# Keeping the adapted feed-forward weights in DRAM for their second use, and splitting the last expert block around the attention before it

## The chip, the core and the metric

The kernel runs on one core of a Trainium2 chip. The metric is the device time of one execution in microseconds, as the median of several runs. All arithmetic is fp32.

## The reference

The kernel computes two layers of a transformer on `x` of 2 x 512 tokens with 512 channels. Each step adds a block of the normalised input to `x`:

```python
x = x + latent_attention_small(layernorm(x))
x = x + ffn_lora(layernorm(x))      # first pass
x = x + gqa(layernorm(x))
x = x + ffn_lora(layernorm(x))      # second pass, the same weights
x = x + mla(layernorm(x))
x = x + ffn_moe(layernorm(x))       # first pass
x = x + mha(layernorm(x))
x = x + ffn_moe(layernorm(x))       # second pass, the same weights
```

Two of the blocks matter here. The feed-forward block with adapters is

```python
y = x @ weight.T + bias
lo = (x @ A[adapter].T) @ B[adapter].T      # rank 16; the adapter depends on the batch alone
out = y + where(use_lora, lo, 0)
```

As the adapter depends on the batch alone, the kernel adds the product of the two adapter matrices to the weight, once for each of the two batches, and multiplies by that sum. The expert block is

```python
logits = x @ W_router.T                      # 8 experts
probs = softmax(logits); top 2, scaled to sum 1 -> combine (tokens x 8)
h  = einsum('nd,erd->ner', x, A)             # 8 experts x rank 16 = 128 columns
hw = h * combine[:, :, None]
out = x @ W_base.T + b_base + 2 * einsum('ner,eor->no', hw, B)
```

## The kernel before

**Tiling.** `x` stays in SBUF as eight tiles of 128 tokens, `x0` to `x7`; tiles 0 to 3 are batch 0 and 4 to 7 batch 1 (`NT` is 4, `NTILES` 8, `KC` 4 chunks of 128 channels). `layernorm(t)` takes statistics on DVE, an inverse root on POOL (L210, tile `rstd`), the scaled rows `xn` on DVE (L182, two buffers), four transposes on TensorE (L195) and a copy by ACT (L200) into `xT[batch]`. With a `bias` it also issues an addition of the bias to `x[t]` on POOL (L215), after `xn`. Most matrix products go through `chain` (L162), a run of matmuls that accumulate in one PSUM bank. The sums are added to `x` on DVE (L218).

**Banks.** PSUM has eight banks by four names: three `sc`, two `pj`, two `tp` and one `av`. `proj()` takes the `pj` banks in turn, `tr()` the `tp` banks, `sc()` the `sc` banks; `turn()` goes round all of them. A bank can be taken again when the last reader of its tile is done.

**Weights.** Tags of the pool `w` are rings: `w8` has five buffers of 1 MB, `w3` six of up to 384 KB, `bias` one. Loads go through SyncE's queue (SP) in the order of the program; a load waits until the buffer that it is to fill is free, and those behind it wait too.

**The adapted block.** `AdaptedBlock` (L736 on) loads the weight, both adapter matrices and the bias; `adapt(m)` makes one quarter of the adapted weight for both batches: two matmuls of 48 rows by 512 columns (L761) and two additions on DVE (L765). `product(b, t)` is the chain of four matmuls of one token tile. In the first pass the four calls of `adapt` stand in the list `ending` at the end of `attn_latent_small`, between the last steps of that attention; that attention's TensorE order is written by hand. The second pass, `ffn_lora`, makes a second `AdaptedBlock` and adapts again.

**The expert block.** `ffn_moe` is called twice, with loads of its own each time. `front(t)` is a chain of four matmuls of 136 columns into a `pj` bank (128 columns of `h` and the 8 logits) followed by the router's chain: 16 small operations on DVE, from `nmax` (L1360) to `hw` (L1378), with an exponential on ACT (L1362) after the first. The last of them, `hw`, reads the bank. `back(t)` transposes `hw` (L1389), copies it with ACT (L1391), and runs a chain of five 512-column matmuls into an `sc` bank. The loop does `front(t)`, a piece of other work, `layernorm` and `back(t - 1)`. The second call writes the output rows.

**The last attention.** `attn_mha` goes over the two batches: `prepare(b)` projects q and k (`rotated`, four chains each into `pj` banks, followed by ACT L1534, a shuffle and a multiplication on DVE L1536 and L1537, two operations on POOL L1538 and L1539, and scattering DMAs) and the values (four chains into `sc` banks); `core(b)` does scores, softmax, the weighted sum and the output product. `core` stands in a branch on a register. In `prepare(1)` the order of the instructions on each engine is the scheduler's; in `core` TensorE's is written by hand. After `prepare(1)` tiles 0 to 3, which are final by then, are normalised for the second expert block.

Of the kernel before, what the change touches and what calls it, by code (L numbers as in the profile page):

```python
# [31 lines left out]
F32 = mybir.dt.float32  # L32
# [5 lines left out]
B, S, D = 2, 512, 512  # L38
P = 128
NT = S // P  # L40
KC = D // P
# [4 lines left out]
class Block:  # L46


    def __init__(self, ctx, tc, x, out):
        nc = self.nc = tc.nc  # L50
        self.tc = tc
        self.out = out
        pool = lambda name, bufs, **kw: ctx.enter_context(tc.tile_pool(name=name, bufs=bufs, **kw))
        self.const = pool("const", 1)
        self.w = pool("w", 2)
        self.work = pool("work", 2)
        self.small = pool("small", 6)
        self.psum = pool("psum", 2, space=bass.MemoryType.PSUM)
        self.turns = 0
        self.held = None  # L60
        self.coef = None

        self.x = [
            self.const.tile([P, D], F32, tag=f"x{t}", name=f"x{t}") for t in range(NTILES)
        ]
        self.source = x
        self.load_x(0)


        self.room = self.const.tile([P, 4 * KC * S], F32, tag="room", name="room")  # L70
# [313 lines left out]
def attn_latent_small(k, a):  # L384
# [7 lines left out]
    nc, tc = k.nc, k.tc  # L392
    with ExitStack() as ctx:
        lp = ctx.enter_context(tc.tile_pool(name="a", bufs=2))
# [260 lines left out]
        blocks = []  # L655
        last = len(quartets) - 1
        adapt = [lambda m=m: blocks[0].adapt(m) for m in range(KC)]
        feed = [lambda t=t: blocks[0].product(0, t) for t in range(NT)]

        tokens = [lambda t=t: k.layernorm(t, k.turn, back=True) for t in range(NT)]  # L660
# [77 lines left out]
class AdaptedBlock:  # L738
# [5 lines left out]
    def __init__(self, k, a):  # L744
        self.k = k
        self.w = k.load(a["f0_w"], [P, KC, D], "w8", 5)

        self.la = k.load(a["f0_a"], [P, D], "w3", 6)
        self.lb = k.load(a["f0_b"], [P, D], "w3", 6)
        self.bias = k.load_row(a["f0_bias"], D, "bias")  # L750
        k.nc.vector.tensor_scalar(self.la, self.la, k.coef, None, ALU.mult)
        self.adapted = [
            k.w.tile([P, KC, D], F32, tag="w8", name="adapted", bufs=5) for b in range(B)
        ]

    def adapt(self, m):
        k, nc = self.k, self.k.nc
# [13 lines left out]
        k.add_to_x(b * NT + t, ps)  # L771


def ffn_lora(k, a):


    block = AdaptedBlock(k, a)
    for m in range(KC):
        block.adapt(m)
    for t in range(NT):  # L780
        k.add_bias(t, block.bias)
    for b in range(B):
        for t in range(NT):
            block.product(b, t)
            if b == 0:
                k.layernorm(NT + t, k.turn, bias=block.bias)
            else:
                k.layernorm(t, k.turn, back=True)
# [533 lines left out]
        k.release()  # L1322


def ffn_moe(k, a, last=False, beside=lambda t: None):

    nc, tc = k.nc, k.tc
    E, R = 8, 16  # L1330
    with ExitStack() as ctx:
        lp = ctx.enter_context(tc.tile_pool(name="f1", bufs=3))
        w = k.load(a["f1_w"], [P, KC, D], "w8", 5)
        war = k.load(a["f1_ar"], [P, KC, E * R + E], "w3", 6)
        wb = k.load(a["f1_b"], [P, D], "w3", 6)
        bias = k.load_row(a["f1_bias"], D, "bias")
        order = k.load_row(a["c_order"], E, "c_order")

        for t in range(NT):
            k.add_bias(t, bias)  # L1340

        def best(p, name):

            top = k.sm(1, name)
            nc.vector.tensor_reduce(top, p, AX.X, ALU.max)
            cand = lp.tile([P, E], F32, tag="cand", name="cand")
            nc.vector.scalar_tensor_tensor(cand, p, top, order, ALU.is_equal, ALU.mult)
            first = k.sm(1, "first")
            nc.vector.tensor_reduce(first, cand, AX.X, ALU.max)
            hot = lp.tile([P, E], F32, tag="hot" + name, name="hot" + name)  # L1350
            nc.vector.tensor_scalar(hot, cand, first, None, ALU.is_equal)
            return top, hot

        def front(t):
            b, cols = t // NT, bass.ts(t % NT, P)
            ps = k.proj()
            k.chain(ps[:, : E * R + E], [(k.xT[b][:, c, cols], war[:, c]) for c in range(KC)])
            logits = ps[:, E * R : E * R + E]
            nmax = k.sm(1, "nmax")
            nc.vector.tensor_reduce(nmax, logits, AX.X, ALU.max, negate=True)  # L1360
            p = lp.tile([P, E], F32, tag="p", name="p")
            nc.scalar.activation(p, logits, AF.Exp, bias=nmax, scale=1.0)  # L1362
            p1, hot1 = best(p, "p1")
            rest = lp.tile([P, E], F32, tag="rest", name="rest")
            nc.vector.scalar_tensor_tensor(rest, hot1, -2.0, p, ALU.mult, ALU.add)
            p2, hot2 = best(rest, "p2")
            both = k.sm(1, "both")
            nc.vector.tensor_tensor(both, p1, p2, ALU.add)
            inv = k.sm(1, "inv")
            nc.vector.reciprocal(inv, both)  # L1370
            c1 = lp.tile([P, E], F32, tag="c1", name="c1")
            nc.vector.tensor_scalar(c1, hot1, p1, None, ALU.mult)
            c2 = lp.tile([P, E], F32, tag="c2", name="c2")
            nc.vector.scalar_tensor_tensor(c2, hot2, p2, c1, ALU.mult, ALU.add)
            comb = lp.tile([P, E], F32, tag="comb", name="comb")
            nc.vector.tensor_scalar(comb, c2, inv, 2.0, ALU.mult, ALU.mult)
            hw = lp.tile([P, E, R], F32, tag="hw", name="hw")
            nc.vector.tensor_tensor(  # L1378
                hw,
                ps[:, : E * R].rearrange("p (e r) -> p e r", e=E),  # L1380
                comb.unsqueeze(2).broadcast_to([P, E, R]),
                ALU.mult,
            )
            return hw

        def back(t, hw):
            b, cols = t // NT, bass.ts(t % NT, P)
            tp = k.tr()
            nc.tensor.transpose(tp[:, :P], hw.rearrange("p e r -> p (e r)"), k.ident)  # L1389
# [8 lines left out]
        rows = {}  # L1398
        for t in range(NTILES + 1):
            if t < NTILES:  # L1400
                rows[t] = front(t)
                beside(t)
            if t < NT:
                k.layernorm(NT + t, bias=bias)
            if t > 0:
                back(t - 1, rows.pop(t - 1))
            if t > NT and not last:
                k.layernorm(t - 1 - NT)


class CausalBound:
# [79 lines left out]
        pool.memset(self.nm[i // 4][:, i % 4], 0.0)  # L1491


def attn_mha(k, a, exact, rooms):

# [8 lines left out]
    with ExitStack() as ctx:  # L1504
# [43 lines left out]
        def prepare(b):  # L1548
            rotated(b, wq, bq, q, (nc.sync, nc.sync))
            if b == 0:  # L1550
                for t in range(NT, NTILES):
                    k.layernorm(t, bias=bo)
            last = rotated(b, wk, bk, kk, (nc.sync, nc.scalar))

            with tc.issue_after(last):
                values(b)
# [135 lines left out]

        for b in range(B):
            prepare(b)
            if b:

                for t in range(NT):
                    k.layernorm(t)
            with tc.If(exact != 0) as branch:
                core(b, True)  # L1700
            with branch.Else():
                core(b, False)
# [3 lines left out]
def kernel(ctx: ExitStack, tc: tile.TileContext, a: dict, out: bass.AP):  # L1706
# [2 lines left out]
    block = attn_latent_small(k, a)  # L1709
    bound = CausalBound(k, a)  # L1710
    attn_gqa(k, a, bound, block)
    ffn_lora(k, a)
    attn_mla(k, a)
    with k.tc.tile_pool(name="heads", bufs=1) as pool:
        rooms = HeadRooms(k, a, pool)
        ffn_moe(k, a, beside=rooms.fill)
        attn_mha(k, a, bound.register(), rooms)
    ffn_moe(k, a, last=True)

# [154 lines left out]
```

## Time and profile before

| what | us |
|---|---|
| median of 3 runs | 2096.95 |
| lowest and highest | 2095.71, 2101.05 |
| the profiled execution, its own time | 2095.05 |
| the profiled execution, span from first to last instruction | 2093.0 |

The mean granted clock of TensorE in that execution is 0.992 of full speed. In the profile PE is TensorE's matmuls, PEld its weight loads, DVE the vector engine, ACT the scalar engine, POOL GpSimd and SP the queue of SyncE. A timeline row gives the start, the duration, the engine, the line of the kernel, the operation, output and inputs by the program's names, the shapes and the number of merged records; in brackets stands how long the engine was idle before and what released it. An fp32 matmul leaves two records, so a chain of four is shown as x8. A row of waits gives the engine and line that waited, what it waited for, the total in us, how often, and the longest.

### The profile page before, as it was taken

To read this page: it belongs to the slowest core of one execution; us is meant where nothing else is said; L and a number is where in the kernel's file an instruction comes from. 1 tells how busy PE (TensorE), PEld (TensorE's weight loads), DVE (VectorE), ACT (ScalarE), POOL (GpSimd) and SP (SyncE) were. 2 spreads that over 40 slices of the span, in tenths; PEclk is the share of its full clock that TensorE was granted. 3 is DMA by queue.
4 is the path that set the end of the run, shared out by engine and by line. 5 is a ranking of instruction groups with operands and counts; after the bars stand their busy time and mean duration, and the time that the engine had idled before them with its cause. 6 is when DMAs were issued, how large, how long until landed. Compare 5 with 4: busy or idle time off the path is not lost. (4 is left out here: it accounts for less than half of the span.)

```text
span 2093.0 us, 40127 instructions
## 1 busy us (share of the span) xinstructions
PE 2028.5 (97%) x15560; PEld 1152.4 (55%) x15560; DVE 1354.0 (65%) x3575; ACT 741.2 (35%) x2072; POOL 969.1 (46%) x1239
## 2 busy tenths in 40 slices
PE   9999999999999999999999989999999989999998
PEld 5544435666666566666665534545454444554654
DVE  6788756656665466566765556666666784846845
ACT  1665632222232222222232145444544311541631
POOL 1101026675656467666653256555555545215220
PEclk9999999999999999999999999999999999999999
DMA  3001022222222222222220321010101003002001
GB/s 110 6 21 41 1 71 71 76 72 71 91 73 77 84 71 76 77 93 77 74 75 20 117 62 55 21 54 22 51 22 52 2 6 71 2 2 41 2 2 41
DMA packets 70220, 107.43 MB, mean 51 GB/s; under 512 B 13698, under 2 KB 50690, under 8 KB 63236
## 3 DMA queue, kind: packets, MB, share of 16 engines
q1 hardware_dynamic: 69380, 103.71, 15.8%
q8 instruction: 126, 2.06, 0.4%
q10 hardware_dynamic: 640, 1.05, 0.3%
q14 instruction: 74, 0.61, 0.1%
HBM read 80.61 MB, written 2.10 MB: 40 GB/s over the span
## 5 line engine op out<-in xcount | busy, mean ns | idle before, releaser
L263 ACT ACTIVATE room<-room,nmax 128x128 f32<-128x128 f32 (+3 forms) x384 | 212.1, 554 | 483.5 <-DVE nmax L253 482.1
L274 POOL TENSOR_SCALAR room<-room,invs 128x128 f32<-128x128 f32 (+3 forms) x384 | 197.4, 533 | 142.2 <-DVE invs L271 142.2
L314 PE MATMUL sc<-turned,vals 32*128 32x128 f32 (+7 forms) x1034 | 187.9, 415 | 1.3 <-DVE turned L287 1.3
L314 PE MATMUL pj<-turned,vals 32*128 32x384 f32 (+7 forms) x708 | 186.6, 425 | 0.0
L210 POOL TENSOR_TENSOR rstd<-ve,mhalf 128x1 f32<-128x1 f32 x80 | 45.6, 574 | 249.6 <-DVE ve L208 230.8
L314 PE MATMUL tp<-turned,vals 32*128 32x256 f32 (+7 forms) x770 | 149.0, 423 | 3.0 <-DMA vals<-v 2.1
L242 PE MATMUL sc<-kT,q 128*32 128x256 f32 (+4 forms) x1528 | 134.0, 384 | 6.8 <-DVE invs L271 4.1
L287 DVE STREAM_TRANSPOSE turned<-room 128x1152 f32<-128x1152 f32 x80 | 109.1, 1363 | 42.1 <-POOL room L274 39.8
L314 PEld LDWEIGHTS sc<-turned,vals 32*128 32x128 f32 (+1 forms) x1034 | 120.3, 168 | 14.4 <-issue 4.4
L958 POOL TENSOR_TENSOR q<-q,cosq 128x512 f32<-128x512 f32 x60 | 89.4, 1489 | 60.2 <-DVE t L955 60.2
L162 PE MATMUL sc<-w,room 128*128 128x512 f32 (+1 forms) x256 | 112.3, 583 | 0.0
L314 PEld LDWEIGHTS pj<-turned,vals 32*128 32x128 f32 (+1 forms) x708 | 104.7, 170 | 4.1 <-issue 1.6
L314 PEld LDWEIGHTS tp<-turned,vals 32*128 32x128 f32 (+1 forms) x770 | 98.2, 170 | 11.5 <-issue 5.7
L218 DVE TENSOR_TENSOR x<-sc,x 128x512 f32<-128x512 f32 x79 | 54.2, 686 | 74.5 <-PE sc L162 69.6
L162 PE MATMUL sc<-w,ctxT 128*128 128x512 f32 x224 | 101.5, 596 | 0.0
L568 PE MATMUL sc<-qm,keys 32*128 32x512 f32 x206 | 96.8, 628 | 0.0
L274 POOL TENSOR_SCALAR probs<-probs,invs 128x128 f32<-128x128 f32 (+3 forms) x128 | 65.7, 532 | 64.7 <-DVE invs L271 60.8
L242 PE MATMUL tp<-kT,q 128*32 128x512 f32 (+4 forms) x984 | 91.7, 407 | 3.8 <-DVE invs L271 3.8
L263 ACT ACTIVATE probs<-probs,nmax 128x128 f32<-128x128 f32 (+3 forms) x128 | 71.1, 556 | 65.3 <-DVE nmax L253 64.0
L253 DVE CUSTOM_DVE_ANT_0 room<-sc,mask 128x256 f32<-128x256 f32 (+3 forms) x149 | 70.7, 475 | 35.8 <-PE sc L242 34.2
L242 PE MATMUL pj<-kT,q 128*32 128x288 f32 (+3 forms) x968 | 89.6, 404 | 2.9 <-POOL q L1226 1.9
L959 POOL TENSOR_TENSOR q<-q,t 128x512 f32<-128x512 f32 x64 | 88.0, 1375 | 6.5 <-DVE q L958 2.5
(615 smaller groups left out, 6174.1 us busy)
## 6 DMA issues: line engine op xcount, KB each, us to landing
w<-in_b_wq SPq DMA_DIRECT2D x16, 1024.0 KB, 4.8
w<-in_b_wo SPq DMA_DIRECT2D x16, 1024.0 KB, 5.6
vals<-v SPq DMA_DIRECT2D x256, 64.0 KB, 2.0
w<-in_m_wo SPq DMA_DIRECT2D x8, 1024.0 KB, 6.6
w<-in_b_wk SPq DMA_DIRECT2D x16, 256.0 KB, 2.6
w<-in_b_wupv SPq DMA_DIRECT2D x16, 256.0 KB, 2.5
w<-in_f_w SPq DMA_DIRECT2D x4, 1024.0 KB, 5.7
w<-in_m_wqn SPq DMA_DIRECT2D x8, 384.0 KB, 3.2
```

The source lines that it names most:

```text
L162: last = self.nc.tensor.matmul(out, lhsT, rhs, start=(i == 0), stop=(i == len(pairs) - 1))
L210: self.nc.gpsimd.tensor_tensor(r, ve, self.mhalf, ALU.pow)
L218: self.latest = self.nc.vector.tensor_tensor(self.x[t], ps, self.x[t], ALU.add).ins
L242: nc.tensor.matmul(ps[32 * i : 32 * i + 32, a - lo : b - lo], q[:, at : at + 32], keys[:, a:b], start=True, stop=True,)
L253: nc.vector.tensor_tensor_reduce(out=row, in0=ps[:, :kv], in1=self.mask_back[:, :kv] if qt % 2 else self.mask[:, S - kv :], op0=ALU.add, o ...
L263: nc.scalar.activation(row, row, AF.Exp, bias=nmax, scale=-1.0, accum_out=total[:, qt : qt + 1])
L274: self.nc.gpsimd.tensor_scalar(row, row, inv[:, qt : qt + 1], 1.0, ALU.mult, ALU.mult)
L287: self.nc.vector.transpose(out[:, :last], probs[:, :last])
L314: self.nc.tensor.matmul(out[:, :, :n], values(i, j), rhs, start=(j == blocks[0]), stop=(j == stop[i]),)
L568: nc.tensor.matmul(ps, keys[b][rows[g], bass.ts(kc, P)], qm[u][rows[g]], start=True, stop=True)
L958: mul.tensor_tensor(q, q, tables["cosq"], ALU.mult)
L959: nc.gpsimd.tensor_tensor(q, q, t2, ALU.add)
```

## The change

The adapted weights are stored to DRAM once (`keep`, two DMAs of 1 MB from POOL's queue after the last `adapt` of the first pass) and read back in the second pass (`again`, two DMAs on SP). The second pass no longer loads the weight and the adapter matrices and no longer adapts.

The expert block becomes an object, `Experts`, which lives from before the first expert block to the end. Its weights, router matrix and order row are loaded once; its pool has two buffers where it had three, and `hw` four. `first` is the old loop of the first call. The second call is split: `begin` stands inside `prepare(1)`, between the projections of q and k, and does `layernorm` and `front` of tiles 0 to 3; `end` stands after the attention, with TensorE's order written by hand: `back(0)`, then in turn `layernorm` of tiles 4 to 7, the other backs of batch 0 and the fronts of batch 1, and at last the four backs of batch 1. The normalisation of tiles 0 to 3 after `prepare(1)` goes.

```diff
@@ attn_latent_small
         adapt = [lambda m=m: blocks[0].adapt(m) for m in range(KC)]
+        adapt[-1] = lambda: (blocks[0].adapt(KC - 1), blocks[0].keep())
@@ AdaptedBlock
+    def keep(self):
+        k = self.k
+        self.kept = [
+            k.dram.tile([P, KC, D], F32, tag=f"kept{b}", name=f"kept{b}") for b in range(B)
+        ]
+        for b in range(B):
+            k.nc.gpsimd.dma_start(out=self.kept[b], in_=self.adapted[b])
+
+    def again(self, bias):
+        k = self.k
+        self.adapted = self.buffers()
+        for b in range(B):
+            k.nc.sync.dma_start(out=self.adapted[b], in_=self.kept[b])
+        self.bias = k.load_row(bias, D, "bias")
@@ ffn_lora
-    block = AdaptedBlock(k, a)
-    for m in range(KC):
-        block.adapt(m)
+    block.again(a["f0_bias"])
@@ Experts (was ffn_moe)
-        lp = ctx.enter_context(tc.tile_pool(name="f1", bufs=3))
...
-            hw = lp.tile([P, E, R], F32, tag="hw", name="hw")
+            hw = lp.tile([P, E, R], F32, tag="hw", name="hw", bufs=4)
...
+    def begin(self):
+        self.added = self.bias()
+        for t in range(NT):
+            self.k.layernorm(t, bias=self.added)
+            self.front(t)
+
+    def end(self):
+        k = self.k
+        with k.tc.manual_schedule(engines={mybir.EngineType.PE}):
+            for t in range(NT + 1):
+                if t < NT:
+                    self.back(t, True)
+                    k.layernorm(NT + t, bias=self.added)
+                if t > 0:
+                    self.front(NT + t - 1)
+            for t in range(NT):
+                self.back(NT + t, True)
@@ attn_mha, prepare
             if b == 0:
                 for t in range(NT, NTILES):
                     k.layernorm(t, bias=bo)
+            else:
+                experts.begin()
             last = rotated(b, wk, bk, kk, (nc.sync, nc.scalar))
...
             prepare(b)
-            if b:
-
-                for t in range(NT):
-                    k.layernorm(t)
@@ tile_hybrid_kernel
-        ffn_moe(k, a, beside=rooms.fill)
-        attn_mha(k, a, bound.register(), rooms)
-    ffn_moe(k, a, last=True)
+    with k.tc.tile_pool(name="f1", bufs=2) as own:
+        experts = Experts(k, a, own)
...
+            experts.first(rooms.fill)
+            attn_mha(k, a, bound.register(), rooms, experts)
+        experts.end()
```

More of the change, by code (lines that the diff above doesn't have):

```diff
@@ L57, in __init__ @@
         self.small = pool("small", 6)
+        self.dram = pool("dram", 1, space=bass.MemoryType.DRAM)
         self.psum = pool("psum", 2, space=bass.MemoryType.PSUM)
@@ L751, in __init__, with buffers @@
         k.nc.vector.tensor_scalar(self.la, self.la, k.coef, None, ALU.mult)
-        self.adapted = [
-            k.w.tile([P, KC, D], F32, tag="w8", name="adapted", bufs=5) for b in range(B)
-        ]
+        self.adapted = self.buffers()
+    def buffers(self):
+        return [
+            self.k.w.tile([P, KC, D], F32, tag="w8", name="adapted", bufs=5) for b in range(B)
+        ]
+    def keep(self):
[7 more added lines that the diff above has]
+        k = self.k
+        self.adapted = self.buffers()
+        for b in range(B):
+            k.nc.sync.dma_start(out=self.adapted[b], in_=self.kept[b])
+        self.bias = k.load_row(bias, D, "bias")
     def adapt(self, m):
@@ L771, in product, with ffn_lora @@
         k.add_to_x(b * NT + t, ps)
-def ffn_lora(k, a):
-    block = AdaptedBlock(k, a)
-    for m in range(KC):
-        block.adapt(m)
+def ffn_lora(k, a, block):
+    block.again(a["f0_bias"])
     for t in range(NT):
@@ L1322, in attn_mla, with __init__ @@
         k.release()
[L1325 to L1331, printed above, removed]
-        lp = ctx.enter_context(tc.tile_pool(name="f1", bufs=3))
+class Experts:
+    def __init__(self, k, a, lp):
+        nc = k.nc
+        E, R = 8, 16
+        self.k, self.a = k, a
+        self.rows = {}
         w = k.load(a["f1_w"], [P, KC, D], "w8", 5)
@@ L1335, in ffn_moe @@
         wb = k.load(a["f1_b"], [P, D], "w3", 6)
-        bias = k.load_row(a["f1_bias"], D, "bias")
         order = k.load_row(a["c_order"], E, "c_order")
-        for t in range(NT):
-            k.add_bias(t, bias)
         def best(p, name):
@@ L1383, in front, with back @@
             )
-            return hw
-        def back(t, hw):
+            self.rows[t] = hw
+        def back(t, last):
+            hw = self.rows.pop(t)
             b, cols = t // NT, bass.ts(t % NT, P)
@@ L1396, in back, with bias, first @@
                 nc.sync.dma_start(out=k.out[t], in_=k.x[t])
-        rows = {}
+        self.front, self.back = front, back
+    def bias(self):
+        return self.k.load_row(self.a["f1_bias"], D, "bias")
+    def first(self, beside):
+        k, bias = self.k, self.bias()
+        for t in range(NT):
+            k.add_bias(t, bias)
         for t in range(NTILES + 1):
             if t < NTILES:
-                rows[t] = front(t)
+                self.front(t)
                 beside(t)
@@ L1405, in ffn_moe @@
             if t > 0:
-                back(t - 1, rows.pop(t - 1))
-            if t > NT and not last:
+                self.back(t - 1, False)
+            if t > NT:
                 k.layernorm(t - 1 - NT)
+    def begin(self):
+        self.added = self.bias()
+        for t in range(NT):
+            self.k.layernorm(t, bias=self.added)
+            self.front(t)
+    def end(self):
[7 more added lines that the diff above has]
+                    self.front(NT + t - 1)
+            for t in range(NT):
+                self.back(NT + t, True)
 class CausalBound:
@@ L1491, in fill, with attn_mha @@
         pool.memset(self.nm[i // 4][:, i % 4], 0.0)
-def attn_mha(k, a, exact, rooms):
+def attn_mha(k, a, exact, rooms, experts):
     nc, tc = k.nc, k.tc
@@ L1694, in attn_mha @@
             prepare(b)
-            if b:
-                for t in range(NT):
-                    k.layernorm(t)
             with tc.If(exact != 0) as branch:
@@ L1711 @@
     attn_gqa(k, a, bound, block)
-    ffn_lora(k, a)
+    ffn_lora(k, a, block)
     attn_mla(k, a)
-    with k.tc.tile_pool(name="heads", bufs=1) as pool:
-        rooms = HeadRooms(k, a, pool)
-        ffn_moe(k, a, beside=rooms.fill)
-        attn_mha(k, a, bound.register(), rooms)
-    ffn_moe(k, a, last=True)
+    with k.tc.tile_pool(name="f1", bufs=2) as own:
+        experts = Experts(k, a, own)
+        with k.tc.tile_pool(name="heads", bufs=1) as pool:
+            rooms = HeadRooms(k, a, pool)
+            experts.first(rooms.fill)
+            attn_mha(k, a, bound.register(), rooms, experts)
+        experts.end()
 def _kmajor(w):
```

## The prediction

> **What bounds the kernel now.** I read the page first, then the windows around the three places that the change touches, then the waits and the timeline inside them. The page's first row of engines says that TensorE is the kernel:
>
> ```profile
> PE 2028.5 (97%) x15560; PEld 1152.4 (55%) x15560; DVE 1354.0 (65%) x3575; ACT 741.2 (35%) x2072; POOL 969.1 (46%) x1239
> ```
>
> With 64 us of idle TensorE in 2093, a change pays only if it takes TensorE instructions away or closes one of its few gaps, and it costs what gaps it opens. The windows show one such gap at the end and none where the second copy of the gap's work is to go (columns: PE, PEld, DVE, ACT, POOL busy, granted clock, DMA share, GB/s):
>
> ```profile
> 1881.00:1925.10 44.10, 43.44 (x113) 19.82 (x111) 22.54 (x45) 7.20 (x12) 28.83 (x23) 1.00 0.33 48
> 2030.80:2052.00 21.20, 12.75 (x39) 7.76 (x38) 13.33 (x50) 1.75 (x5) 7.17 (x8) 0.68 0.00 1
> 2052.00:2093.00 41.00, 36.92 (x131) 19.79 (x129) 21.77 (x104) 3.92 (x15) 0.00 (x0) 0.99 0.14 52
> ```
>
> The first is `prepare(1)` of the last attention (TensorE full), the other two are the last expert block. The waits of the last 63 us name the gap: normalised rows, then the router's chain on DVE.
>
> ```profile
> PE tp L195 <- DVE xn L182: 4.3, 1, 4.3
> PE tp L1389 <- DVE first L1349: 4.2, 1, 4.2
> ```
>
> The timeline has the durations that I use:
>
> ```profile
> 1139.33 1.12 PE L761 MATMUL tp<-w,w 48*128 48x512 f32 x2 [0.79 <-ACT ctxT L329]
> 1140.94 3.70 PE L162 MATMUL sc<-w,ctxT 128*128 128x512 f32 x8
> ...
> 1154.87 0.69 PE L761 MATMUL pj<-w,w 48*128 48x512 f32 x1
> ...
> 1157.64 3.70 PE L162 MATMUL tp<-adapted,room 128*128 128x512 f32 x8
> ...
> 2041.86 1.19 DVE L1365 SCALAR_TENSOR_TENSOR rest<-hotp,p 128x8 f32<-128x8 f32 x1
> 2041.76 1.26 POOL L215 TENSOR_TENSOR x<-x,bias 128x512 f32<-128x512 f32 x1 [0.95 <-DVE xn L182]
> ...
> 2046.53 3.62 PE L162 MATMUL sc<-w,room 128*128 128x512 f32 x4
> ...
> 2079.03 1.09 PE L162 MATMUL pj<-w,room 128*128 128x136 f32 x8
> 2079.95 0.27 PE L1389 MATMUL tp<-ident,hw 128*128 128x128 f32 x1
> ...
> 2084.36 0.27 PE L1389 MATMUL tp<-ident,hw 128*128 128x128 f32 x1
> 2084.47 3.60 PE L162 MATMUL sc<-w,room 128*128 128x512 f32 x8
> ```
>
> The reader is to see four things. The adapting matmuls take 1139.33 to 1140.94 and 1154.87 to 1157.64. A 128x8 DVE operation that takes 0.17 us alone (2046.51) takes 1.19 beside a POOL addition and ends when that ends. A front is 0.92 us of TensorE (2079.03 to 2079.95), front and back together 5.33 (2079.03 to 2084.36), so a back is 4.41. And four records at 2046.53 take what eight take at 2084.47: after a gap the clock is half.
>
> **Part 1, adapted weights kept.** The eight adapting matmuls of the second pass go: 1.61 + 2.77 = 4.38 us of TensorE. In the built order two matmuls of `product(0, 0)` stand where the first two adapting ones stood, so that spot does not fall idle. The eight additions (0.68 each) were beside TensorE. **-4.4 us.**
>
> Added: two 1 MB stores on POOL's queue after the last adapting sum (278.19), ahead of `rstd` at 283.57. No row shows a DMA issued by POOL. From below: 0.33 us each, SP's issue row. From above: the Trainium skill, "SBUF — State Buffer", section on the bandwidth-pool intuition, says POOL writes its descriptors through a port that DVE can hold, and that a 0.62 us transfer took 3.1 beside a DVE copy. That speaks against this change, and 2 x 3.1 would free POOL at 284.4, 0.8 us after `rstd` is due. I take 1 us each, nearer SP's row since DVE stands idle from 278.2 to 281.6. By either value nothing is late: the normalised rows made from that `rstd` at 284.15 are first transposed at 301.63, 17 us later. Buffers: the weights that follow into the first copy are requested at 297.02, the stores (5.7 us landing for 1 MB, row `w<-in_f_w`) are out by about 290. On SP the reload of batch 0 takes the slot of `w<-in_f_w` (issued 1052.97); that of batch 1 stands behind the last value spread (issued 1089.75, 11.24 us), so about 1101, landing about 1107. Behind it wait only the latent attention's loads, which move up a buffer. Needed at 1139 and 1166: **0**, with 30 us of cover.
>
> **Part 2, four fronts moved from the end into `prepare(1)`, and the end ordered by hand.** At the end TensorE begins with `back(0)` at once: `front(0)` ran straight on from the last output matmul at 2030.85 in the old trace, so the branch costs it nothing. Then: back 4.4 (2035.3), stall 0.5 for the rows of tile 4 (ready 2035.7), transposes 0.44, back 4.4, transposes, front 0.92, back, transposes, front, back, transposes, two fronts, four backs. Total: 8 x 4.4 + 4 x 0.92 + 4 x 0.44 + 0.5 = 41.2, so the last matmul ends at about 2072.1 instead of 2088.9. `hw(6)` is ready at about 2060, needed at 2063.3, so no wait. **-16.8 us**; two idle stretches and the slow clock go.
>
> In `prepare(1)`, in built order: q projection, 8 transposes, fronts 0 and 1, 8 transposes, fronts 2 and 3, k projection, values. All fronts and projections share the two `pj` banks, and a front holds its bank until `hw`, the last of 16 DVE operations. So front 2 waits for `hw(0)`, and k's first chain for `hw(2)`: TensorE stands behind two router chains in a row, with k and the values queued behind it.
> - q ends at 1894.9, fronts 0 and 1 at 1898.4.
> - On DVE the chain stands behind q's four rotations and two `xn`. They alternate with POOL's additions (1.27 each), as one holds out the other; two bias additions (2 x 1.27) now lie between q's rotations. Stepping through: the last rotation ends at 1902.2.
> - First pair: four POOL operations are left and each holds up one DVE step (5.5 us to 1907.7, with nine steps done); the next 15 take 2.1 us, as 1685.84 to 1687.76 shows for 13: `hw(0)` 1910.0, `hw(1)` 1911.6.
> - Fronts 2 and 3 at the slow clock, 1.9 each: 1910.05 to 1913.8. Second pair, POOL idle, a single chain being 3.5 us (2064.17 to 2067.67): `hw(2)` 1916.7, `hw(3)` 1918.3.
> - k and values: `prepare(0)` took 27.7 us from k's first chain to the first score (1747.9 to 1776.1 less transposes).
> - Clock: "TensorE: Matmul & The Clock Gate", part 1, gives half speed for one window of 3.4 us: 1.7 lost. Here a gap of 2.27 us (1930.8) was followed by about 4.5 slow ones to 1938, so I take 2.2, by the row; the sum by the rule would be 0.5 lower.
>
> Core 1 starts at 1916.75 + 27.5 + 2.2 = 1946.5 instead of 1925.1: **+21.4 us**, of which 3.7 are the fronts. q's and k's scatters stay covered, as in `prepare(0)`, where no wait follows the values. The weights, router and bias loads that are dropped from the second expert block were early: 0. The pool of two buffers instead of three changes no engine's order in the first block: 0.
>
> **Sum.** -4.4 - 16.8 + 21.4 = +0.2 on the profiled execution's 2095.05, which is 1.9 below the median of the runs, 2096.95. So about **2097**. A difference under 0.3% (6.3 us) is about what a measurement of this kernel can't tell from none.
>
> **The rivals.**
> - *A, the banks come free earlier* (0.18). If DVE gets past POOL's additions without alternating, the first pair ends 5 us sooner; with the slow clock also spared (2.2), core 1 starts at about 1939.3, +14 instead of +21.4: about -7 in all, **2090**. [...] Against: the row of 1.19 above. It decides if k's chain starts before about 1912.
> - *B, slower: the router chains don't interleave* (0.24). The place is the two `pj` banks. If the chains run one after another on DVE, `hw(2)` comes at 1902.2 + 5.5 (POOL) + 3 x 3.5 + 3.8 (two slow fronts) = 1922, and with 4.5 us lost to the clock core 1 starts at 1954: +7.7 in all, **2105**. For it: single chains in the first expert block take their 3.5 us each, and every hop over ACT costs 0.35 to 0.5. Against: the built order interleaves them. It decides if k starts after about 1922.5.
> - *C, the copy doesn't save* : if an adapting matmul only filled the wait of 0.79 at 1139, 0.8 of the 4.4 is lost. It shifts the sum and changes no sign, so it has no chance of its own.
>
> **How the numbers follow.** The forecast has 0.58, its own range 2091 to 2103. Range: 2088.5 to 2106, a little beyond A's and B's times; under 2 in 10 is left out. Chances: faster 0.18 (A), within 0.3% 0.58, slower 0.24 (B).
>
> **What would show it.** Adapting matmuls at one place only; no wait of TensorE for `adapted`. From the last q matmul to the first of k: about 22 us, with two waits of TensorE for `hw` (9 and 3 us) and a clock well under 1.00. From the first k matmul to the first score about 30. From the last output matmul to the last matmul about 41.5 instead of 58.5, with no wait over 1 us. Wrong would be: a wait for the reloaded weights, a wait of POOL's `rstd` near 284 that reaches TensorE, or k starting outside 1912 to 1922 (of the old clock, less 4.4).

## The result, and the profile after

| | us |
|---|---|
| before, median of 20 runs (lowest, highest) | 2096.70 (2093.85, 2101.32) |
| after, median of 20 runs (lowest, highest) | 2092.65 (2090.14, 2096.93) |
| ratio after to before, 95% interval | 0.9981 (0.9974 to 0.9987) |
| profiled execution, span before and after | 2093.0, 2089.6 |

The forecast was about 2097, no change. The kernel became 4.05 us faster. That lies inside the range (2088.5 to 2106) and within the 0.3% that were called no change, but it is 4.4 us away from the number given, and the interval, 2.7 to 5.5 us less, excludes no change: 20 runs tell much less apart than the 0.3% (6.3 us) that the forecast took for the limit. The runs of several kernels here fall into two groups some 4 us apart (of the changed kernel's 20, 15 lie from 2090.1 to 2094.3 and 5 from 2095.4 to 2096.9), so a median of a few runs can shift by a microsecond or two; the durations of single stages are steadier, and the argument below rests on them.

The page's first row of engines, after. TensorE is busy 7.6 us less than before (2028.5):

```profile
PE 2020.9 (97%) x15544; PEld 1149.4 (55%) x15544; DVE 1347.5 (64%) x3566; ACT 742.3 (36%) x2072; POOL 973.3 (47%) x1241
```

The same windows as before, now of the changed kernel: `prepare(1)` from the first q matmul to the first score of core 1, and the end from the first `back` to the last matmul (columns: length, PE, PEld, DVE, ACT, POOL busy, granted clock, DMA share, GB/s):

```profile
1876.16:1938.91 62.75, 51.28 (x145) 25.81 (x143) 34.68 (x108) 8.50 (x16) 31.10 (x24) 0.89 0.24 34
2043.60:2085.60 42.00, 41.07 (x137) 20.95 (x135) 22.17 (x88) 5.34 (x16) 7.20 (x8) 1.00 0.12 44
```

`prepare(1)` was 44.1 us at 1.00 and full; it is 62.75 at 0.89 with 11.5 us of idle TensorE. The end has one gap of 0.9 us left and no slow clock. The waits of TensorE from 1870 to 2092:

```profile
PE pj L163 <- DVE cand L1365: 10.3, 2, 7.7
...
PE tp L196 <- DVE xn L183: 1.7, 2, 0.9
```

The first row is the price: two waits, 10.3 us, of chains into a `pj` bank for a router chain on DVE. (The profile names `cand`, the last instruction of DVE that it saw end; what frees the bank is `hw`, just before it.) The timeline of TensorE in `prepare(1)`, with q's four chains, fronts 0 and 1, fronts 2 and 3, k, the values:

```profile
1876.16 13.90 PE L163 MATMUL pj<-room,w 128*128 128x512 f32 x32
...
1891.37 2.12 PE L163 MATMUL pj<-w,room 128*128 128x136 f32 x16 [0.44 <-ACT room L201]
...
1903.31 3.75 PE L163 MATMUL pj<-w,room 128*128 128x136 f32 x16 [7.72 <-DVE cand L1365]
1909.58 15.67 PE L163 MATMUL pj<-room,w 128*128 128x512 f32 x32 [2.53 <-DVE cand L1365]
1925.09 13.90 PE L163 MATMUL sc<-w,room 128*128 128x512 f32 x32
```

The rows of part 1 in the changed kernel are these. Two matmuls of the first product stand where two adapting matmuls stood, and no wait for `adapted` follows; on POOL the two stores take 1.34 us together, and the next `rstd` is not late (283.35, and 283.57 before):

```profile
1140.43 1.98 PE L163 MATMUL tp<-adapted,room 128*128 128x512 f32 x4 [0.79 <-ACT ctxT L330]
...
1155.99 1.88 PE L163 MATMUL tp<-adapted,room 128*128 128x512 f32 x4
```

```profile
277.68 1.34 POOL L768 DMA_DIRECT2D kept<-adapted  x2 [84.54 <-DVE adapted L786]
283.35 0.56 POOL L211 TENSOR_TENSOR rstd<-ve,mhalf 128x1 f32<-128x1 f32 x1 [4.33 <-DVE ve L209]
```

And of the end, its only wait of some size and the end of its last chain:

```profile
2049.08 0.63 PE L196 MATMUL tp<-ident,xn 128*128 128x128 f32 x4 [0.90 <-DVE xn L183]
...
2084.55 1.02 PE L163 MATMUL sc<-w,hT 128*128 128x512 f32 x2
```

Where the 4 us came from is seen best in stages between two rows of TensorE's timeline that both kernels have. Each number is a difference of two starts (the last column: from the start of the last output chain to the end of the last matmul); the other kernels are the experiments below:

| kernel | second feed-forward pass | latent attention | output chain of core 0 to first score of core 1 | core 1, scores to last values | end |
|---|---|---|---|---|---|
| before | 46.58 | 495.01 | 47.43 | 88.87 | 61.94 |
| before, a second profile | 46.58 | 495.94 | 47.43 | 88.14 | 61.28 |
| after | 42.01 | 493.12 | 66.18 | 88.27 | 45.39 |
| kept weights alone | 42.01 | 495.17 | 47.43 | 89.13 | 62.23 |
| expert block alone | 46.59 | 495.07 | 65.96 | 88.35 | 45.41 |
| other banks | 42.01 | 493.76 | 53.84 | 90.77 | 45.37 |
| additions in core 1 | 42.01 | 493.88 | 63.94 | 88.24 | 45.38 |
| fronts behind k | 42.01 | 494.40 | 53.30 | 90.60 | 45.39 |
| waits filled | 42.00 | 493.09 | 63.38 | 89.17 | 45.55 |
| front 3 in `pj`, scatters on SP | 42.01 | 494.21 | 51.85 | 88.92 | 45.57 |
| front 3 in `pj`, scatters on both | 42.00 | 492.32 | 50.18 | 90.62 | 45.39 |

The three stages that the change touches gave -4.57, +18.75 and -16.55, together -2.4 us. They repeat to 0.4 us in the kernels that share them (66.0 to 66.3 for `prepare(1)`, 45.4 to 45.6 for the end; the end of before, with its gap, to a microsecond). The forecast had -4.4, +21.4 and -16.8.

### The profile page after: what moved, and what is told of

The parts are those of the page before. It is cut to its first block, busy times and chain, and to the rows that moved or that the text cites. A ratio compares the mean times of both kernels' runs of the same rounds, so it can differ in the third digit from the quotient of the medians.

```text
span 2089.6 us, 40080 instructions
## 1 busy us (share of the span) xinstructions
PE 2020.9 (97%) x15544; PEld 1149.4 (55%) x15544; DVE 1347.5 (64%) x3566; ACT 742.3 (36%) x2072; POOL 973.3 (47%) x1241
## 5 line engine op out<-in xcount | busy, mean ns | idle before, releaser
L315 PEld LDWEIGHTS tp<-turned,vals 32*128 32x128 f32 (+1 forms) x770 | 98.8, 170 | 10.7 <-issue 4.9
```

Of the source, the lines that this page charges most:

```text
L315: self.nc.tensor.matmul(out[:, :, :n], values(i, j), rhs, start=(j == blocks[0]), stop=(j == stop[i]),)
```

## The experiments

The question was which step of the sum was off, and what sizes the 18.75 us. My theory after the traces: TensorE stands behind `hw` in the two `pj` banks; how long is set by POOL additions that hold router steps on DVE, and by the slow clock after the waits. Rivals: DVE and POOL are simply full there, and freeing banks moves the wait elsewhere; or the surplus gain is part 1's.

### The two parts, each alone

```diff
 # kept weights alone: the kernel before, and
+        adapt[-1] = lambda: (blocks[0].adapt(KC - 1), blocks[0].keep())
...
-    block = AdaptedBlock(k, a)
-    for m in range(KC):
-        block.adapt(m)
+    block.again(a["f0_bias"])
```

> The kept adapted weights alone, the last expert block as before. If part 1 is worth its TensorE time and no more, as the prediction's first step has it (eight adapting matmuls, 4.4 us): 4.0 to 5.0 us less than before, about 2092.3, the first q matmul of prepare(1) about 4.4 to 4.9 us earlier than before's 1881.12 and everything after it at before's distances. Rival 'the surplus is part 1's': the changed kernel came out about 3.5 us lower than the sum of its steps because the kept weights also close a wait that the sum left out; then 7.5 to 8.5 us less, about 2089. Rival 'the adapting only filled a wait': less than 3.6 us.

Measured: 2091.12 us against 2095.95, ratio 0.9968 (0.9957 to 0.9979). The medians are 4.8 us apart, and the stage is 4.57 shorter (46.58 to 42.01). The ratio's interval, 4.4 to 9.0 us, takes in the rival's 7.5 to 8.5 too, so the times alone don't decide. The trace does: part 1 is worth its TensorE time, and no other stage of this execution is shorter than in before, so there is no closed wait of 3 us. A gain of a microsecond elsewhere it can't exclude (see below).

> The expert block as one object alone, the weights adapted again in the second pass. By the prediction's terms (+21.4 in prepare(1), -16.8 at the end): +4.6 us against before. By the terms as the changed kernel's trace has them (+18.8, -16.6, core 1 -0.6): +1.6 us. Rival 'the surplus is part 1's': prepare(1) would here cost what was forecast, +4 or more. Two parts that don't interact must give, with the kept weights alone, the changed kernel's -4.

This is the changed kernel with the `-` lines of the diff above in place of its `+` lines. Measured: 2097.35 against 2095.95, ratio 1.0003 (0.9995 to 1.0011). That is +1.4 by the medians, and the interval (-1.0 to +2.3 us) excludes the +4.6 of the prediction's own terms. Its `prepare(1)` costs 18.53 and its end gains 16.53. So no interaction of the two parts shows: -4.8 and +1.4 give -3.4, where both together gave -4.05. Of the surplus over the forecast, 3.2 us sit in the expert block's terms and 0.4 in part 1's.

### Where the fronts' sums are kept

```diff
-        def front(t):
+        def front(t, bank=k.proj):
...
-            ps = k.proj()
+            ps = bank()
...
 # begin
-            self.front(t)
+            self.front(t, self.k.av if t == 3 else self.k.sc)
```

> The changed kernel, with the four fronts of prepare(1) in banks sc, sc, sc, av instead of the two pj banks, so that neither a later front nor k's projection waits for hw. Theory 'the banks' (what prepare(1) costs beyond its 3.7 us of fronts is TensorE standing behind hw in two pj banks): the two waits of 7.7 and 2.5 us for the router chains go, fronts 2 and 3 wait only for their normalised rows (copied by ACT at about 1898), k starts at about 1900.5 instead of 1909.6, and the kernel is 7 to 11 us faster than the changed one, about 2083. It would be less than 9 only if k's rotations, now behind the same router chains on DVE, land after the values are done. Rival 'the vector engines' (DVE and POOL together are what is full in prepare(1), and TensorE's wait only shows it): the wait moves to the first score, for ks, and the gain is under 3 us.

Measured: 2081.48 us, ratio to before 0.9926 (0.9913 to 0.9940), 10.7 us below the repeat of the changed kernel that ran beside it (next section). TensorE's timeline:

```profile
1899.24 1.19 PE L163 MATMUL sc<-w,room 128*128 128x136 f32 x8 [2.34 <-ACT room L201]
...
1901.20 12.22 PE L163 MATMUL pj<-room,w 128*128 128x512 f32 x28
...
1928.82 0.34 PE L1641 MATMUL sc<-ks,qs 32*128 32x128 f32 x1 [1.26 <-DMA ks<-room]
```

Fronts 2 and 3 now wait only for ACT's copies, at nearly full speed (1.19 and 1.09 us), and k starts at 1901.20 instead of 1909.58. The stage falls from 66.18 to 53.84. The last row is the beginning of a new limit: k's rotations stand behind the same router chains on DVE, so the first scores wait for `ks` (1.26 us, and 0.4 once more), and core 1 takes 2.5 us more than in the changed kernel. The theory of the banks holds; the rival's mechanism exists, but 10 us further down.

### What sizes the wait: POOL's additions

> The changed kernel, with the four bias additions of POOL moved from between q's rotations to after the values of prepare(1) (same sums). The prediction held that POOL additions stand between q's rotations and then each hold a router step on DVE. Theory 'the shared lock sizes the stall': POOL's last rotation addition ends about 2.5 us earlier (two bias additions of 1.26 lie after 1895.96), hw(0) with it, k starts about 2 to 3 us earlier, and the kernel is 2 to 3 us faster than the changed one, about 2090. Rival 'only the router's own length' (32 chained small DVE steps): within 0.5 us of the changed kernel.

Measured: 2092.14 us, ratio 0.9974 (0.9964 to 0.9984), and a stage of 66.31. This edit did nothing: nothing held the additions back, the scheduler put them at the same places of POOL's queue (1896.22 and 1899.11), and every engine's order is that of the changed kernel. It says nothing of the additions' part. It serves as a repeat of the changed kernel beside the other runs, 3.8 us below before. The edit that moves them puts them behind the branch:

```diff
 # begin
-            self.k.layernorm(t, bias=self.added)
+            self.k.layernorm(t)
 # core(b, causal), first lines
+            if b:
+                for t in range(NT):
+                    k.add_bias(t, experts.added)
```

> The changed kernel with the four bias additions of prepare(1) made at the beginning of core(1), where the branch keeps them (the run before left them at the same places of POOL's queue: its order was that of the changed kernel). Theory 'the shared lock sizes the stall': without the additions that stand at 1895.96 and 1898.85, POOL's last rotation addition ends at about 1898.6 instead of 1901.3, no router step is held after that, hw(0), fronts 2 and 3 and k all come 2 to 3 us earlier, first score about 2 to 3 us earlier after the last output chain (63.5 instead of 66.2 us), and the kernel is 2 to 3 us below the changed one. At most 0.5 us of it is given back in core(1). Rival 'only the router's own length': 66 us stay, within 0.5 us of the changed kernel.

Measured: 2091.10 us, ratio 0.9972 (0.9960 to 0.9984); 5.3 us below the runs of before beside it, where the repeat was 3.8 below its own. That is 1.5 us of gain by the medians, where 2 to 3 were expected, and the two ratios overlap; the times alone don't show it. The stage does: it fell from 66.18 (66.31 in the repeat) to 63.94, about as expected. First the changed kernel, DVE from the last rotation on, and then POOL:

```profile
1894.79 1.75 DVE L1586 TENSOR_TENSOR t<-t,w 128x512 f32<-128x512 f32 x1
...
1897.15 0.54 DVE L1365 SCALAR_TENSOR_TENSOR cand<-p,p,c_order 128x8 f32<-128x8 f32 x1
1897.72 0.16 DVE L1367 TENSOR_REDUCE first<-cand 128x1 f32<-128x8 f32 x1
1897.80 0.15 DVE L1363 TENSOR_REDUCE p<-p 128x1 f32<-128x8 f32 x1
1897.92 0.99 DVE L1369 TENSOR_SCALAR hotp<-cand,first 128x8 f32<-128x8 f32 x1
1898.95 1.18 DVE L1383 SCALAR_TENSOR_TENSOR rest<-hotp,p 128x8 f32<-128x8 f32 x1
1900.05 1.30 DVE L1390 TENSOR_SCALAR c<-hotp,p 128x8 f32<-128x8 f32 x1
...
1902.87 0.29 DVE L1396 TENSOR_TENSOR hw<-pj,comb 128x128 f32<-128x128 f32 x1
```

```profile
1895.96 1.71 POOL L216 TENSOR_TENSOR x<-x,bias 128x512 f32<-128x512 f32 x1
1897.63 1.26 POOL L1587 TENSOR_TENSOR room<-room,w 128x512 f32<-128x512 f32 x1
1898.85 1.26 POOL L216 TENSOR_TENSOR x<-x,bias 128x512 f32<-128x512 f32 x1
1900.07 1.26 POOL L1588 TENSOR_TENSOR room<-room,t 128x512 f32<-128x512 f32 x1
```

Three router steps of 128x8 elements take 0.99, 1.18 and 1.30 us, and each ends within 0.02 us of the end of a POOL operation (1898.89, 1900.11, 1901.33). Before them `cand` takes 0.54 and ends with the POOL operation that is already under way (1897.67). With the two bias additions gone, two of these four POOL operations are left. `cand` takes 0.54 as before, one step is held after it, and the next takes 0.17:

```profile
1898.39 1.12 DVE L1369 TENSOR_SCALAR hotp<-cand,first 128x8 f32<-128x8 f32 x1
1899.54 0.17 DVE L1383 SCALAR_TENSOR_TENSOR rest<-hotp,p 128x8 f32<-128x8 f32 x1
```

TensorE follows, 1.5 to 1.6 us earlier although this execution had begun `prepare(1)` 0.6 later; its first wait is 5.75 instead of 7.72:

```profile
1901.80 3.63 PE L163 MATMUL pj<-w,room 128*128 128x136 f32 x16 [5.75 <-DVE cand L1365]
1907.95 15.67 PE L163 MATMUL pj<-room,w 128*128 128x512 f32 x32 [2.52 <-DVE cand L1365]
```

So each POOL addition that stands in the router's way adds about 1.1 us to the wait.

### What sizes the rest: the slow clock

```diff
 # begin
             self.k.layernorm(t, bias=self.added)
+            if t == 2:
+                self.fill(76)
             self.front(t)
+        self.fill(24)
+
+    def fill(self, n):
+        bank = self.k.sc()
+        for i in range(n):
+            self.k.nc.tensor.transpose(bank[:, bass.ts(i % 4, P)], self.k.ident, self.k.ident)
```

> The changed kernel with 100 transposes of the identity (read by nothing) in prepare(1)'s two waits for hw: some 75 before front 2, some 24 before front 3 and k, at about 0.11 us each. It prices the slow clock after the waits. Theory 'the clock term' (of the +18.8: fronts 2 and 3 take 3.75 us for what takes 1.9 at full clock, and k 15.67 for what takes 13.9): both come back in part, from the last output chain to the first score 63 to 64.5 us instead of 66.2, the kernel 1.5 to 3.5 us below the changed one. Rival 'the slow matmuls cost nothing, since DVE's router chains would end no sooner': 66 us stay; if the transposes overrun the waits, up to 1 us more.

Measured: 2090.35 us, ratio 0.9969 (0.9957 to 0.9981), and a stage of 63.38, 2.80 less:

```profile
1902.23 1.17 PE L163 MATMUL pj<-w,room 128*128 128x136 f32 x8 [1.24 <-DVE cand L1365]
...
1904.51 1.19 PE L163 MATMUL pj<-w,room 128*128 128x136 f32 x8
...
1907.50 13.90 PE L163 MATMUL pj<-room,w 128*128 128x512 f32 x32
```

With the waits filled by transposes that nobody reads, fronts 2 and 3 take 1.17 and 1.19 us instead of 3.75 together, and k takes 13.90 instead of 15.67. Front 2 starts as late after q as in the changed kernel (27.1 us in both), and still 2.8 us come back. The clock term is real. k's share of it is 1.77 us. The other 1.0 is k's earlier start: front 2 ends sooner, but its router chain also runs ahead of front 3's on DVE instead of in turn with it, and this run doesn't part the two. In the changed kernel the granted clock shows k's share as well (columns as in the windows above):

```profile
1909.60:1912.00 2.40, 2.40 (x4) 1.12 (x5) 1.18 (x7) 0.00 (x0) 0.00 (x0) 0.61 0.22 22
1912.00:1914.50 2.50, 2.50 (x5) 0.98 (x5) 0.00 (x0) 0.00 (x0) 0.00 (x0) 0.69 0.00 0
1914.50:1917.00 2.50, 2.50 (x8) 1.06 (x7) 1.11 (x3) 0.69 (x1) 0.32 (x1) 1.00 0.00 0
```

0.39 of 2.40 us and 0.31 of 2.50 are 1.7 us lost. That is what the rule in the Trainium skill's "TensorE: Matmul & The Clock Gate", part 1, gives as an estimate (half of one window of about 3.4 us), rather than the 2.2 that I took from another gap's row.

### The kernel before, profiled again

> The kernel before, unchanged, for a second profile: how far the stages that the change does not touch differ from one execution to the next. In the profiles so far the latent attention takes 493.1 to 495.2 us and the grouped one 868.9 to 870.2. If the second half of the gain (4.0 measured, 2.4 by the three stages that the change touches) is such scatter, this profile's latent attention may lie anywhere between 493 and 495.2. If the kept weights shorten it, it lies at 495, as in both kernels that adapt twice.

Measured: 2095.51 us in one run. The latent attention takes 495.94 us, so the three executions that adapt twice lie at 495.0 to 495.9, and those with kept weights (with those of the next section) at 492.3 to 495.2, one at 498.1. The waits of TensorE for other engines in that stage are alike; the differences are tenths, spread over all of it. A gain of about a microsecond from the kept weights is possible there, but not shown: three executions stand against eleven, and their ranges overlap.

### Nothing of TensorE behind a router chain

The layer norms stay between q and k, the fronts go behind k, ahead of the values.

```diff
 # front takes a bank, as above; begin: only the layer norms
-            self.front(t)
...
 # a new method
+    def fronts(self):
+        k = self.k
+        for t, bank in enumerate((k.tr, k.tr, k.av, k.sc)):
+            self.front(t, bank)
 # prepare
             with tc.issue_after(last):
+                if b:
+                    experts.fronts()
                 values(b)
```

> The changed kernel with the normalised rows of tiles 0 to 3 where they are, but the four fronts behind k's projection, in banks tp, tp, av, sc: nothing of TensorE is queued behind a router chain, and k's rotations go ahead of the router on DVE and POOL. Theory 'the banks, and what is queued behind them': prepare(1) costs its 3.7 us of fronts and no more; from the last output chain to the first score about 51 us (47.4 before, 66.2 in the changed kernel), core 1 then starts about 15 us earlier and the kernel is about 15 us faster than the changed one, 2077. Between: if k's scatters land late, as in the run with other banks (1.6 us of waiting for ks), 13. Rival 'the vector engines are full in prepare(1)': the wait moves to ks or to the values' banks, and no more than the 10.7 us of the run with other banks come back.

Measured: 2081.20 us, ratio 0.9927 (0.9913 to 0.9940), a stage of 53.30: no better than the other banks, where 15 us had been expected. Its waits from 1876 to 1960:

```profile
PE tp L196 <- DVE xn L183: 2.7, 2, 1.9
...
PE sc L1647 <- DVE hw L1396: 0.8, 1, 0.8
```

2.7 us go to transposes that stand in front of most of k and wait for `xn`. The last row, with 0.4 us more for `vs`, is at the first scores: the order on DVE had put the last two router chains behind the values' additions, because their exponentials stood behind the issue of four scatters on ACT's queue (1914.10 to 1917.71).

> The run with the fronts behind k, with what was left in its trace taken out: the transposes of tiles 2 and 3 go behind k's second chain (they waited 1.9 and 0.8 us for xn), k's scatters all go to SP's queue (on ACT's they stood ahead of the router's exponentials of tiles 2 and 3, so the last two router chains ended at 1928.9, behind the values, and the first maxima of core(1) behind them), and the four bias additions are made in core(1). Theory 'the banks, and what is queued behind them': prepare(1) costs its 3.7 us of fronts: from the last output chain to the first score about 51 us (53.3 in that run), and core(1) up to its last values is back at 88 to 89 us (90.6). Together 4 us less than that run, about 2077, so 15 us below the changed kernel. Rival 'the vector engines are full': core 1 waits for ks or nm instead, and less than 1.5 us come back.

> As the run before, with half of k's scatters left on ACT's queue. It tells the two repairs apart. If the exponentials behind four transfers' issue (3.6 us on ACT) were what kept the last router chains behind the values: about 51 us to the first score, but core(1) keeps the 2 us more (90.6 instead of 88.5), about 2079. If the transfers' place on ACT costs nothing: as the run before within 0.5 us.

Measured: 2085.43 us, ratio 0.9940 (0.9925 to 0.9954), with a stage of 56.88; and with ACT's queue kept 2081.98, ratio 0.9933 (0.9917 to 0.9948), a stage of 53.33. Both expectations of the stage and the time failed; of the second, that core 1 keeps its 2 us held (90.61). The wait for `xn` is gone in both, and with the scatters on SP core 1 is back at 88.26 us, but a new wait took more, the longest of these:

```profile
PE sc L163 <- DVE vs L1632: 4.7, 1, 4.7
```

The third value chain waits for an `sc` bank, 4.7 us (2.9 with ACT's queue): front 3 holds one of the three, and `vs`, which frees the others, stands behind router chains on DVE. It is the mechanism of the changed kernel again, with other banks.

```diff
-        for t, bank in enumerate((k.tr, k.tr, k.av, k.sc)):
+        for t, bank in enumerate((k.tr, k.tr, k.av, k.proj)):
```

> The run with all of k's scatters on SP's queue, with front 3 in a pj bank (free once k's third chain is copied) instead of sc: in that run the third value chain stood 4.7 us for a sc bank, since front 3 held one and vs came behind the router chains on DVE. With all three sc banks for the values, only the fourth chain waits for the first vs. Theory 'the banks': the 4.7 us become about 1.5, core(1) stays at 88 to 89 us, from the last output chain to the first score 52 to 53.5 us instead of 56.9. Rival 'DVE's queue is what is full': the fourth chain waits as the third did, and less than 1.5 us come back.

> The same bank for front 3, with half of k's scatters on ACT's queue, where three of the vs stand ahead of the last two router chains on DVE. Theory 'the banks': no value chain waits (the fourth would start at about 1919.8, the first vs is done at about 1919.3), the wait of 2.9 us goes, about 50.5 us to the first score, which is before's 47.4 and not quite the 3.7 us of the four fronts; core(1) keeps its 2 us, because its first maxima stand behind the last router chains: about 2079, 13 us below the changed kernel. Rival: 53 us stay.

Measured: 2077.43 us, ratio 0.9910 (0.9897 to 0.9924), a stage of 51.85 and one wait of 1.4; and 2077.56, ratio 0.9916 (0.9902 to 0.9929), a stage of 50.18 with core 1 at 90.62. In the second, TensorE runs from k through the last fronts and the values without a wait:

```profile
1907.65 1.09 PE L163 MATMUL pj<-w,room 128*128 128x136 f32 x8
1908.58 13.90 PE L163 MATMUL sc<-w,room 128*128 128x512 f32 x32
```

Both are 18 us below before and some 15 below the changed kernel, the fastest of the study; which of the two is faster the runs don't tell. In the second the fronts cost the stage 2.75 us (50.18 less 47.43), less than their 3.7 us of matmuls, since before had short gaps there (0.5 us for `xn`, for one), and core 1 pays 1.75 (90.62, and 88.87 in before). In the first the stage pays 4.4 and core 1 nothing. Either way it is 4.5.

## Why the prediction was right and wrong

**Right: part 1.** -4.4 was forecast and the stage gave -4.57, in each kernel with kept weights. Stores on POOL and reloads on SP cost nothing that a profile shows: a store took 0.67 us of issue (1.34 for two), where 1 had been taken from between 0.33 and 3.1, and TensorE has no wait for `adapted`.

**Right: the end.** -16.8 forecast, -16.55 measured. TensorE waited 0.90 for the first transposes, where 0.5 was taken, and nowhere else. That the two differ by only 0.25 is in part luck: the old end itself took 61.28 in the second profile of before and 61.94 in the first.

**Right in kind: the two waits.** Two waits for `hw` of 9 and 3 us were forecast, 7.72 and 2.53 measured; fronts 2 and 3 3.8 us, measured 3.75; the interleaved router chains (`hw` of tile 0 starts at 1902.87, of tile 1 at 1904.32) exclude rival B. Rival A would have needed k before 1912 of the old clock. k started at 1909.58, which with the 4.96 us that the kernel was early by then is 1914.5: between the two, inside the forecast's own 1912 to 1922. The additions did hold router steps, as the forecast said against A; only the reductions beside them were not held (0.16 and 0.15).

**Wrong: the size of prepare(1), +21.4 for +18.75.** The mechanism was there; the step that failed is the sum that leads to `hw(0)` at 1910.0, from which everything after it was counted. It came at 1908.1 of the old clock, 1.9 us sooner, because three of its terms were each too long. The last rotation ended at 1901.5, where 1902.2 had been said: 0.7. Then "four POOL operations are left and each holds up one DVE step (5.5 us to 1907.7...)": four were left, but the first had already begun under the rotation and held only part of one step (`cand`, 0.54), so POOL was done at 1906.3, after 4.8 us: 0.7. The nine steps that were to be done by then were done, and the next fifteen took 1.8 us to the end of `hw(0)`, where 2.3 had been said: 0.5. Most of this lies in the stretch that the forecast took them from, 1685.84 to 1687.76, where two `hotp` steps take 0.71 together; here they take 0.35. From `hw(0)` to k's start it took 6.4 us, 6.75 had been said: 0.3. From k to the first score it took 29.3 instead of 29.7: 0.4, which is the clock term taken as 2.2 where k lost 1.77. Together these make the 2.6. The run with the additions in core 1 confirms the price of one held step, about 1.1 us. Why the last rotation ended earlier than stepped through is not shown. (The sum took 27.5 us for k and the values where the line above it has 27.7; measured without the slow clock it was 27.6.)

**Not in the sum: 1.7 us.** With the terms as measured the sum is -2.4 and the medians differ by 4.05. In the two profiled executions the stages that the change doesn't touch add -1.0 (latent attention -1.9, grouped attention +1.3, core 1 -0.6, the rest +0.2). This may be scatter or a small gain of the kept weights; it stays open. With the right sizes the forecast would have been about 2094.5, a change of -2.4 instead of +0.2: the sign of so small a sum hung on its largest term.

## What to carry to other kernels

When work is moved into a stage where TensorE is full, ask first which banks its results hold and until when: a chain of small vector steps that ends in the bank's last reader costs little of TensorE's own time, but everything queued behind the next use of that bank. Here 3.7 us of matmuls cost 18.75 us in the stage with their sums in two shared banks; other banks alone brought that to 6.4, other banks and another order to 2.75, and the same stall came back when a bank was taken without asking who else takes it. The next stage has to be counted too: in two of these runs core 1 took 1.75 to 1.9 us more than before. A sum of terms with opposite signs is only as good as its largest term; trace that one's vector steps one by one.

## What was not expected of the hardware

The clock of TensorE can stay at half in one execution at a place where it is full in another, while TensorE works. At the beginning of the latent attention TensorE has short waits (up to 1.03 us). Two windows of the first run with all scatters on SP (front 3 in `sc`), where that attention took 498.06 us, and then the same two of the changed kernel, where it took 493.12 (columns as in the windows above):

```profile
1220.00:1225.00 5.00, 5.00 (x7) 1.18 (x5) 0.92 (x8) 1.45 (x5) 0.00 (x0) 0.50 0.15 36
1225.00:1230.00 5.00, 5.00 (x8) 1.63 (x8) 1.34 (x3) 0.22 (x1) 2.51 (x2) 0.50 0.21 50
```

```profile
1220.00:1225.00 5.00, 5.00 (x11) 1.67 (x11) 2.37 (x11) 1.66 (x5) 0.27 (x2) 1.00 0.14 33
1225.00:1230.00 5.00, 3.81 (x57) 2.12 (x59) 1.56 (x7) 2.61 (x7) 3.77 (x3) 1.00 0.22 52
```

In the first execution TensorE is busy all of the time from 1220 to 1230 at a granted clock of 0.50; in the second the clock is 1.00, and TensorE is already ahead. Both kernels have the same instructions there and reach the place within 0.5 us of each other. The first leaves it some 4 us later. Why the clock fell in one execution and not in the other no run here shows, nor how often it does.

An addition on POOL held small DVE steps, 128x8 elements, until it ended, three times in a row (0.99, 1.18 and 1.30 us for what takes 0.17 to 0.22 alone). Two reductions beside the first of these additions were not held (0.16 and 0.15).
